# Two transformer layers on one core: another order of the seven products, of the score heads and of TensorE's work in the second attention

## The chip, the cores and the metric

The kernel runs on one core of a Trainium2 chip. The metric is the device time of one execution in microseconds; the time before is the median of three runs. All data are fp32, and every fp32 matmul stands in the trace as two records.

## What is computed

Two pre-norm layers, each an attention and a gated FFN, on x of shape (4, 256, 256): batch B = 4, 256 positions, D = 256. Both attentions have 16 heads of 128.

```python
x = x + L0_attn(layernorm(x))   # sliding window of 128, RMS norm of q and k, RoPE, 8 kv heads
x = x + L0_ffn(layernorm(x))    # silu(x w_gate) * (x w_up), 2 of every 4 units kept, w_down
x = x + L1_attn(layernorm(x))   # causal, no rotation: q, k, v from W_Q, W_K, W_V, out by W_O
x = x + L1_ffn(layernorm(x))    # fwht(silu(x W1) * (x W3)) W2, hidden 1024
```

The change touches the third line and, by a shared generator, the fourth.

## The kernel before

**Steps.** The second attention (`attention1`) works in units of one group of four heads and one batch: unit n = 4g + b, n = 0 to 15. `pipelined` runs three stages over them with lags 0, 1 and 2: in step s it emits `project(s)`, then `score(s - 1)`, then `attend(s - 2)`, so steps run from 0 to 17. After these it calls the functions listed for the step in `behind` (weights of the output projection prepared in steps 1, 5 and 8; FFN work in 0 and from 11 on).

**Project.** Each projection (q and k together as `qk`, and `v`) is a product of 2x2 blocks done with seven block products (Strassen-Winograd) in place of eight. The generator `seven_products` (L643) emits them: product number i adds to one of three PSUM accumulators x, y and z, and after each one an engine reads the accumulator. ScalarE (ACT) copies into the SBUF tiles u0, u1 and u2, or VectorE (DVE) adds a u to the accumulator and writes a block of the result: c11 from z and u0, c12 from y and u2, c22 from x and u1; c21 is ScalarE's copy of x at the end. The accumulators are never cleared between products on the same one, so a product on x must wait until the copy or sum that reads x is through. Below, "x6" is product 6 on accumulator x, and so on. `project1` (L828) runs three such generators in turn, one product of each: qk (four matmuls of 128 columns, L835), v (one of 256, L841) and, for units 4 to 12, `between`: a product of the output projection of the unit four before (`out_by_seven`, matmuls L772, sums L777 on VectorE). These are called the steps with a projection between; steps 0 to 3 and 13 to 15 have none.

**Score and attend.** `score` calls `probabilities` for two pairs of heads. Per head it has two score matmuls (L213 and L214) into a bank, reductions with mask and maximum on VectorE (L216), then by pair the bias nb (L221), four exponentials on ScalarE (L226), the sums' reciprocal rs (L231) and the scaling on GpSimd (POOL, L234). `planes` splits the result into 16-bit planes on POOL (L240) and transposes them by a DMA from SyncE's queue (L249) into plT. `attend` joins the planes into pT (L260: one half on ScalarE, behind c21's copy; the other on VectorE, behind `last_of["sum"]`), multiplies with v (`values`, L268 and L271, into the bank av), and ScalarE copies av into zT (L735). POOL makes sums of zT for the output projection.

**Banks.** The pool `ps1` has four banks in rotation. The four score banks, the two av banks, v's accumulator x and the projection's `po1` share it, so av0 takes a bank that a score had four allocations earlier.

**The second FFN** (`ffn1`) uses `seven_products` too, in eight rounds of half a hidden layer; `gated1` (L906, matmuls L912) puts the down projection's products (`between`) after the fourth and the sixth of the seven products. VectorE makes its weight differences t_gu in steps 14 and on.

**What sets the order.** A scheduler places the instructions of each engine's queue by priorities and its own estimates; source order is its guide and not binding. Each engine then works through its queue in order. In the second attention it had moved part of the scores and av matmuls of steps 1 to 3 and 13 to 15 ahead of products that come earlier in the source: one score head ahead of x4 in steps 1, 3, 13, 14 and 15, and in step 2 three scores ahead of x6 and one ahead of x4, with av matmuls in part before x4 and behind the next step's first product. In steps 4 to 12 TensorE's queue follows the source.

Of the kernel before, what the change touches and what calls it, by code (L numbers as in the profile page):

```python
# [20 lines left out]
F32 = mybir.dt.float32  # L21
# [3 lines left out]
ALU = mybir.AluOpType  # L25
# [3 lines left out]
B, T, D = 4, 256, 256  # L29
# [19 lines left out]
def two_layers(ctx, tc, consts, tables, x, wq, wkv, wo, w_gate, w_up, w_down,  # L49
               w_k, w_q, w_v, w_o, w1, w3, w2, out):  # L50
    nc = tc.nc
# [27 lines left out]
    def page(name):  # L79

        return work.tile([P, 4, T], F32, tag="page", name=name, bufs=8)
# [9 lines left out]
    mask1 = cst[:, C_M1:]  # L91
# [52 lines left out]
    last_of = {}  # L144
# [121 lines left out]
    def values(v0, v1, pT, av):  # L266

        nc.tensor.matmul(  # L268
            av, lhsT=v0, rhs=pT[:, 0:T], start=True, stop=False, skip_group_check=True
        )  # L270
        nc.tensor.matmul(  # L271
            av[:, P:T], lhsT=v1, rhs=pT[:, T : 3 * P], start=False, stop=True,
            skip_group_check=True,
        )
# [21 lines left out]
        xt = xs[b * NT + t]  # L296
        nc.vector.tensor_tensor(xt, po, xt, ALU.add)

    def pipelined(stages, lags, behind, order):


        done, held, depth = {}, {}, max(lags) + 1
        for step in range(B * 4 + depth - 1):
            for k in order:
                n = step - lags[k]
                if 0 <= n < B * 4:
                    held[n] = stages[k](n, held.get(n))
                    if stages[k] is stages[-1]:
                        done[n] = held.pop(n)
            for fn in behind.get(step, ()):  # L310
                fn(done)


    def attention0():
# [328 lines left out]
    def seven_products(product, x, z, y, c11, c12, c21, c22, shape, z_alone=True):  # L643


        u = [late.tile(shape, F32, tag="u", name="u", bufs=4) for _ in range(3)]
        product(y, 5, True)
        nc.scalar.copy(u[1], y)
        yield
        product(x, 1, True)  # L650
        nc.scalar.copy(u[0], x)
        yield
        product(z, 2, z_alone)
        nc.vector.tensor_tensor(c11, z, u[0], ALU.add)
        yield
        product(x, 6, False)
        nc.scalar.copy(u[2], x)
        yield
        product(y, 3, False)
        nc.vector.tensor_tensor(c12, y, u[2], ALU.add)  # L660
        yield
        product(x, 7, False)
        last_of["sum"] = nc.vector.tensor_tensor(c22, x, u[1], ALU.add)
        yield
        product(x, 4, False)
        last_of["copy"] = nc.scalar.copy(c21, x)  # L666
        yield
# [23 lines left out]
    def attention1(finish_ffn0):  # L691
        left = left1

        def project(n, _):
            g, b = divmod(n, 4)
            if b == 1 and 1 <= g < 3:
                load_group1(g + 1)
            held = project1(left[b], gw[g], out_by_seven(n - 4) if 4 <= n < 13 else None)
            if g == 0 and b + 1 < B:
                with tc.issue_after(last_of["sum"].ins):  # L700
                    left[b + 1] = left_of(xn1[b + 1])
            if g == 0 and b + 2 < B:
                xn1[b + 2] = normed(b + 2, by_dma=True)
            return held

        def score(n, held):
            qk, v = held
            ps = [
                probabilities(qk[:, 0], qk[:, 1], (2 * kk, 2 * kk + 1), mask1) for kk in range(2)
            ]  # L710
            return [planes(p, page_of_planes) for p in ps], v

        zTs, kept = {}, {14: (9, 10), 15: (11, 13)}

        def attend(n, held):
            ps, v = held
            for m in kept.get(n, ()):
                out(m, True)(zTs)
            if n in (1, 3, 5, 7):
                zT = late.tile([P, 4, T], F32, tag="zT1", name="zT1", bufs=1)  # L720
            else:
                zT = page("zT1")
            zTs[n] = zT
            for kk in range(2):
                pT = joined(ps[kk], (
                    (
                        (nc.vector.tensor_copy, slice(0, 1), None) if n < 1 else
                        (nc.scalar.copy, slice(0, 1), last_of["copy"])
                    ),
                    (nc.vector.tensor_copy, slice(1, 2), last_of["sum"]),  # L730
                ))
                av = bank([2, T], "av1")
                for j in range(2):
                    values(v[:, 0, 2 * kk + j, :], v[:, 1, 2 * kk + j, :], pT[:, j], av[:, j, :])
                nc.scalar.copy(zT[:, 2 * kk : 2 * kk + 2, :], av)  # L735
            if n < 9:
                z_left[n] = left_of_z(zT, z_sums[:, n % 2])
            return zT

        z_left, w_right = {}, {}  # L740

        def left_of_z(z, s):
            x11, x12, x21, x22 = (
                z[:, 2 * k : 2 * k + 2, t * P : (t + 1) * P] for t in range(2) for k in range(2)
            )
            for i, a, b, op in (
                (0, x21, x22, ALU.add), (1, s[:, 0], x11, ALU.subtract),
                (2, x11, x21, ALU.subtract), (3, x12, s[:, 1], ALU.subtract),
            ):
                nc.gpsimd.tensor_tensor(s[:, i], a, b, op)  # L750
            return x11, x12, s[:, 3], x22, s[:, 0], s[:, 1], s[:, 2]

        def right_of_out(g):
            w, t = gw[g][2], w_sums[:, g % 2]
            w_right[g] = right_of(
                *(w[:, 2 * k : 2 * k + 2, m * P : (m + 1) * P] for k in range(2) for m in range(2)),
                [t[:, i] for i in range(4)],
            )

        def out_by_seven(n):  # L760


            g, b = divmod(n, 4)
            left, right = z_left[n], w_right[g]
            sums = bank([3, P], "po1")
            x, y, z = (sums[:, i, :] for i in range(3))
            for o, i, t, m in (
                (y, 5, 1, 1), (x, 1, 0, 0), (z, 2, 0, 0), (x, 6, 0, 1), (y, 3, 0, 1),
                (x, 7, 1, 1), (x, 4, 1, 0),
            ):  # L770
                for j in range(2):
                    nc.tensor.matmul(  # L772
                        o, lhsT=left[i - 1][:, j, :], rhs=right[i - 1][:, j, :],
                        start=(i == 5 and j == 0), stop=(j == 1), skip_group_check=True,
                    )
                to = xs[b * NT + t][:, m * P : (m + 1) * P]
                nc.vector.tensor_tensor(to, o, to, ALU.add)  # L777
                yield

        def load_ffn1(_):  # L780
            nonlocal w1_sb, w3_sb
            w1_sb = load_ffn(w1, (NC, NF, P), "w1")
            w3_sb = load_ffn(w3, (NC, NF, P), "w3")

        def out(n, kept=False):
            g, b = divmod(n, 4)

            def emit(done):
                if not kept:
                    project_out1(bank([NT, D], "po1"), done[n], gw[g][2], b)  # L790
                else:
                    with tc.issue_after(last_of[1].ins):
                        project_out1(st([P, NT, D], "po1"), done[n], gw[g][2], b)
            return emit

        behind = {step: [lambda _, g=g: right_of_out(g)] for g, step in enumerate((1, 5, 8))}
        behind[0] = [lambda _: finish_ffn0()]
        behind[12] = [load_ffn1]

        def prepare(_):  # L800
            w2h.extend(hadamard(w2_raw))
            w2h[1](_)

        behind.setdefault(11, []).append(prepare)
        for i in range(12):
            behind.setdefault(11 + i // 4, []).append(
                lambda _, i=i: w2h[2][i](last_of["planes"].ins)
            )

        def prepare_ffn1(half):  # L810
            def emit(_):
                with tc.issue_after(last_of["sum"].ins):
                    r_ffn1.append(factors_ffn1(half))
            return emit

        behind.setdefault(14, []).append(prepare_ffn1(0))
        behind.setdefault(15, []).append(out(12))
        behind[16] = behind.get(16, []) + [
            lambda _: xn_f.append(normed(0, by_dma=True)),
            prepare_ffn1(1),  # L820
        ]
        behind[17] = [out(14), out(15)]
        pipelined((project, score, attend), (0, 1, 2), behind, (0, 1, 2))

    def st(shape, name):
        return st_pool.tile(shape, F32, tag="st", name=name)
# [104 lines left out]
    def ffn1():  # L931
# [22 lines left out]
    late = ctx.enter_context(  # L954
        tc.tile_pool(name="late", bufs=2, reuse_waits="tile", side="right")
    )
# [97 lines left out]
```

## Time and profile before

| what | value |
|---|---|
| median of 3 runs (lowest, highest) | 737.86 us (737.40, 738.69) |
| the profiled execution | 738.5 us |
| its span in the trace | 736.7 us |
| first attention and FFN (0 to 352 us): TensorE busy | 345.3 of 352.0 us |
| second attention (352 to 654.6 us): TensorE busy | 300.7 of 302.6 us |
| second FFN (654.6 to 736.7 us): TensorE busy | 79.1 of 82.1 us |
| TensorE clock granted, all three stretches | 1.00 |
| one step with a projection between (431.25 to 449.06) | 17.81 us |

The profile is one execution taken by the hardware profiler. Its page lists the busy time of each engine (PE is the matmuls, PEld the weight loads), the chain of work that ended last, and the costliest groups of instructions. The timeline gives start and length of instructions by engine; a bracket at its end says how long the engine stood idle before and what released it. "L663" is line 663 of the kernel. Ends of matmuls are modelled, so pauses of TensorE are read from start to start.

### The profile page before, as it was taken

The page shows a single profiled execution, that of the slowest core. Times are in us where ns is not written, and L with a number is a line of the kernel's source. Part 1 is how long each engine was busy: PE and PEld are TensorE (multiplying, and loading weights), DVE is VectorE, ACT ScalarE, POOL GpSimd, SP SyncE. Part 2 cuts the span into 40 slices and gives each one's busy share as a digit, 9 for nine tenths or more (in the row PEclk, how much of TensorE's full clock was granted, in tenths as well). Part 3 has the DMA queues.
Part 4 walks back from the last instruction along what each step waited for, and adds up shares of the span by engine and source line. Part 5 has one row for each costly group of instructions (what it writes and reads, how often), then busy time and mean ns, then how long its engine had stood idle before and what let it go on. Part 6 is the DMA issues. An engine that isn't in the chain of part 4 may idle for free.

```text
span 736.7 us, 11967 instructions
## 1 busy us (share of the span) xinstructions
PE 725.1 (98%) x4020; PEld 597.1 (81%) x4020; DVE 485.5 (66%) x1459; ACT 407.6 (55%) x983; POOL 369.8 (50%) x525
## 2 busy tenths in 40 slices
PE   9999999999999999999999999999999999999998
PEld 5556576666666778888998999999998999899997
DVE  6999877888887537987855755575453566464443
ACT  2487887667768952222265555555555666434332
POOL 1588878897799631011127544464446665520000
PEclk9999999999999999999999999999999999999999
DMA  8732344425445545001114433442233522401100
GB/s 323 298 65 51 58 92 82 92 52 93 89 79 98 84 105 182 16 14 24 58 21 82 120 58 44 86 116 44 44 73 44 158 44 44 88 13 23 23 14 30
DMA packets 138350, 57.54 MB, mean 78 GB/s; under 512 B 131504, under 2 KB 133680, under 8 KB 137520
## 3 DMA queue, kind: packets, MB, share of 16 engines
q1 hardware_dynamic: 138288, 56.77, 33.7%
q8 instruction: 32, 0.52, 0.3%
q14 instruction: 30, 0.25, 0.1%
HBM read 22.94 MB, written 1.05 MB: 33 GB/s over the span
## 4 chain that ended last, share of the span: by engine, by line
PE 70%; POOL 9%; DVE 8%; issue 7%; ACT 3%; DMA 2%; SPq 0%; POOLq 0%; DVEq 0%; ACTq 0%
PE pj L446 10%; PE po_f L595 8%; PE pgu L550 8%; PE po L292 7%; PE qk_x L835 4%; PE sc L214 4%; PE gu_x L912 4%; PE av L394 3%; POOL p L234 3%; POOL pl L240 3%; PE po L772 3%; PE qk_y L835 2%; PE sc L213 2%; PE v_x L841 2%; PE gu_y L912 2%
## 5 line engine op out<-in xcount | busy, mean ns | idle before, releaser
L234 POOL TENSOR_SCALAR p<-p,rs 128x128 f32<-128x128 f32 (+1 forms) x256 | 115.9, 470 | 129.2 <-DVE rs L231 124.0
L240 POOL TENSOR_SCALAR pl<-p 128x1536 uint16<-128x1536 uint16 x64 | 94.2, 1472 | 4.5 <-POOL p L234 0.5
L260 ACT COPY pT<-plT 128x1536 uint16<-128x1536 uint16 (+1 forms) x60 | 86.4, 1495 | 12.3 <-DMA plT<-pl 12.3
L216 DVE CUSTOM_DVE_ANT_0 p<-sc,cst 128x128 f32<-128x128 f32 (+1 forms) x256 | 78.9, 352 | 9.4 <-PE sc L214 7.3
L226 ACT ACTIVATE p<-p,nb,r 128x128 f32<-128x128 f32 (+1 forms) x128 | 68.3, 535 | 20.1 <-DVE nb L223 20.1
L226 ACT ACTIVATE p<-p,nb 128x128 f32<-128x128 f32 (+1 forms) x128 | 56.4, 441 | 11.9 <-DVE nb L221 11.9
L446 PE MATMUL pj<-wq,xnT 128*128 128x512 f32 x128 | 61.2, 597 | 1.1 <-DVE qT L508 1.1
L446 PE MATMUL pj<-wkv,xnT 128*128 128x512 f32 x128 | 60.1, 592 | 0.0
L292 PE MATMUL po<-wo,zT 128*128 128x256 f32 x256 | 57.9, 379 | 0.0
L456 ACT ACTIVATE sq<-pj 128x512 f32<-128x512 f32 (+1 forms) x64 | 30.9, 489 | 42.6 <-DVE qc L451 42.2
L292 PEld LDWEIGHTS po<-wo,zT 128*128 128x128 f32 x256 | 48.3, 190 | 7.0 <-ACT kT L519 0.6
L156 POOL TENSOR_SCALAR ve<-mv 128x2 f32<-128x2 f32 (+1 forms) x17 | 4.4, 258 | 95.5 <-DVE mv L152 95.0
L446 PEld LDWEIGHTS pj<-wkv,xnT 128*128 128x128 f32 x128 | 24.3, 190 | 30.2 <-issue 28.5
L666 ACT COPY qk<-qk_x 128x512 f32<-128x512 f32 x16 | 9.4, 586 | 64.7 <-PE qk_x L835 61.1
L451 DVE TENSOR_TENSOR qs<-pj,sin_s 128x512 f32<-128x512 f32 (+1 forms) x64 | 35.3, 552 | 13.5 <-PE pj L446 12.9
L446 PEld LDWEIGHTS pj<-wq,xnT 128*128 128x128 f32 x128 | 23.7, 191 | 24.3 <-issue 20.1
L777 DVE TENSOR_TENSOR x<-po,x 128x128 f32<-128x128 f32 x63 | 18.0, 286 | 35.8 <-PE po L772 35.8
L268 PE MATMUL av<-pT,v 128*128 128x256 f32 x128 | 38.6, 383 | 1.8 <-DVE nb L221 1.1
L240 POOL TENSOR_SCALAR qpl<-qc 128x1024 uint16<-128x1024 uint16 x20 | 28.8, 1450 | 19.1 <-PE av L398 8.3
L214 PE MATMUL sc<-kT,qT 128*128 128x256 f32 x128 | 38.3, 381 | 0.0
L214 PE MATMUL sc<-qk 128*128 128x256 f32 x128 | 38.2, 380 | 0.0
L489 POOL TENSOR_TENSOR r<-ve,mhalf 128x12 f32<-128x12 f32 x16 | 36.6, 2288 | 0.8
(165 smaller groups left out, 1858.0 us busy)
## 6 DMA issues: line engine op xcount, KB each, us to landing
w<-in_w_dram SPq DMA_DIRECT2D x3, 1024.0 KB, 4.7
wq<-in_wq_dram SPq DMA_DIRECT2D x4, 512.0 KB, 7.6
wkv<-in_wkv_dram SPq DMA_DIRECT2D x4, 512.0 KB, 8.2
wo<-in_wo_dram SPq DMA_DIRECT2D x4, 512.0 KB, 10.2
w_qk<-in_w_q_dram SPq DMA_DIRECT2D x4, 512.0 KB, 4.2
w_qk<-in_w_k_dram SPq DMA_DIRECT2D x4, 512.0 KB, 6.0
w_v<-in_w_v_dram SPq DMA_DIRECT2D x4, 512.0 KB, 7.1
w_o<-in_w_o_dram SPq DMA_DIRECT2D x4, 512.0 KB, 5.6
```

Of the source, the lines that this page charges most:

```text
L214: nc.tensor.matmul(sc[:, P : 3 * P], lhsT=q[:, P:T], rhs=k, start=True, stop=True)
L216: last_of["mx"] = nc.vector.tensor_tensor_reduce(out=p[:, j, cols], in0=sc[:, cols], in1=mask[:, cols], scale=1.0, scalar=-3.0e38, op0=ALU ...
L226: last_of["exp"] = nc.scalar.activation(p[:, j, cols], p[:, j, cols], AF.Exp, bias=nb[:, j, i : i + 1], scale=SCALE1 if rq is None else rq ...
L234: nc.gpsimd.tensor_scalar(p[:, j, cols], p[:, j, cols], rs[:, j, i : i + 1], 1.0, ALU.mult, ALU.mult)
L240: last_of["planes"] = nc.gpsimd.tensor_scalar(o, i, 1.0, 1.0, ALU.mult, ALU.mult)
L260: copy(words.rearrange("p (n w) -> p w n", w=2), halves[:, :, js].rearrange("p w j n -> p w (j n)"),)
L292: nc.tensor.matmul(po, lhsT=zTs[hd // 4][:, hd % 4, t * P : (t + 1) * P], rhs=w[:, hd, :], start=(hd == 0), stop=(hd == n - 1),)
L446: last_of[0] = nc.tensor.matmul(pj, lhsT=xnT[:, c, t * P : (t + 1) * P], rhs=w[:, g, c, :], start=(c == 0), stop=(c == NC - 1),)
L550: nc.tensor.matmul(o[:, j, :], lhsT=w[:, c, f0 + j, :], rhs=xnT[:, c, :], start=(c == 0), stop=(c == NC - 1),)
L595: nc.tensor.matmul(pos[b][t], lhsT=hs[n][:, j, t * P : (t + 1) * P], rhs=w[:, 4 * gc + j, :], start=(gc == 0 and j == 0), stop=(gc == 1 an ...
L835: last_of[1] = nc.tensor.matmul(o[:, j, :], lhsT=wqk[i - 1][:, j // 2, j % 2, :], rhs=x[i - 1], start=(first and j == 0), stop=True, skip_ ...
L912: nc.tensor.matmul(o[:, j, :], lhsT=r[j // 2][i - 1][:, j % 2, :], rhs=x[i - 1], start=(first and j == 0), stop=True, skip_group_check=True,)
```

## The change

1. `seven_products`: the order of products goes from 5, 1, 2, 6, 3, 7, 4 (accumulators y x z x y x x) to 1, 5, 6, 3, 7, 2, 4 (x y x y x z x). c11's sum, and with it `last_of["sum"]`, comes sixth. The u tiles of qk and v get tags of their own, three tiles each, in place of one tag with four. `out_by_seven` goes to the same order.
2. `score` takes the head pairs (1, 3) and (0, 2) in place of (0, 1) and (2, 3); `attend` indexes v by the new heads and copies av into every second head of zT.
3. `pipelined` gets `in_order`; the second attention gives (1, 18), which holds TensorE to source order (`tc.manual_schedule`) in steps 1 to 17. The other engines stay with the scheduler.

The queues of the changed kernel, as built: nothing moves on any engine in the first attention and FFN, and SyncE's queue is the same throughout. On TensorE each of steps 1 to 17 is seven products, four scores, four av, in this order. ScalarE and VectorE have their copies and sums in the new order; where the scheduler of before set the reductions of a score between two pT copies (as at 587.50), both pT copies now come first, and in step 16 the reductions come ahead of the pT copies. POOL moves two small norm operations near the end.

```diff
@@ -296,19 +296,26 @@
         xt = xs[b * NT + t]
         nc.vector.tensor_tensor(xt, po, xt, ALU.add)
 
-    def pipelined(stages, lags, behind, order):
+    def pipelined(stages, lags, behind, order, in_order=(0, 0)):
 
 
         done, held, depth = {}, {}, max(lags) + 1
-        for step in range(B * 4 + depth - 1):
-            for k in order:
-                n = step - lags[k]
-                if 0 <= n < B * 4:
-                    held[n] = stages[k](n, held.get(n))
-                    if stages[k] is stages[-1]:
-                        done[n] = held.pop(n)
-            for fn in behind.get(step, ()):
-                fn(done)
+        def steps(numbers):
+            for step in numbers:
+                for k in order:
+                    n = step - lags[k]
+                    if 0 <= n < B * 4:
+                        held[n] = stages[k](n, held.get(n))
+                        if stages[k] is stages[-1]:
+                            done[n] = held.pop(n)
+                for fn in behind.get(step, ()):
+                    fn(done)
+
+        first, last = in_order
+        steps(range(first))
+        with tc.manual_schedule(engines={mybir.EngineType.PE}):
+            steps(range(first, last))
+        steps(range(last, B * 4 + depth - 1))
 
 
     def attention0():
@@ -643,15 +650,13 @@
     def seven_products(product, x, z, y, c11, c12, c21, c22, shape, z_alone=True):
 
 
-        u = [late.tile(shape, F32, tag="u", name="u", bufs=4) for _ in range(3)]
-        product(y, 5, True)
-        nc.scalar.copy(u[1], y)
-        yield
+        tag = "u" if len(shape) == 3 else "uv"
+        u = [late.tile(shape, F32, tag=tag, name="u", bufs=3) for _ in range(3)]
         product(x, 1, True)
         nc.scalar.copy(u[0], x)
         yield
-        product(z, 2, z_alone)
-        nc.vector.tensor_tensor(c11, z, u[0], ALU.add)
+        product(y, 5, True)
+        nc.scalar.copy(u[1], y)
         yield
         product(x, 6, False)
         nc.scalar.copy(u[2], x)
@@ -660,7 +665,10 @@
         nc.vector.tensor_tensor(c12, y, u[2], ALU.add)
         yield
         product(x, 7, False)
-        last_of["sum"] = nc.vector.tensor_tensor(c22, x, u[1], ALU.add)
+        nc.vector.tensor_tensor(c22, x, u[1], ALU.add)
+        yield
+        product(z, 2, z_alone)
+        last_of["sum"] = nc.vector.tensor_tensor(c11, z, u[0], ALU.add)
         yield
         product(x, 4, False)
         last_of["copy"] = nc.scalar.copy(c21, x)
@@ -706,7 +714,7 @@
         def score(n, held):
             qk, v = held
             ps = [
-                probabilities(qk[:, 0], qk[:, 1], (2 * kk, 2 * kk + 1), mask1) for kk in range(2)
+                probabilities(qk[:, 0], qk[:, 1], heads, mask1) for heads in ((1, 3), (0, 2))
             ]
             return [planes(p, page_of_planes) for p in ps], v
 
@@ -731,8 +739,9 @@
                 ))
                 av = bank([2, T], "av1")
                 for j in range(2):
-                    values(v[:, 0, 2 * kk + j, :], v[:, 1, 2 * kk + j, :], pT[:, j], av[:, j, :])
-                nc.scalar.copy(zT[:, 2 * kk : 2 * kk + 2, :], av)
+                    hd = 2 * j + 1 - kk
+                    values(v[:, 0, hd, :], v[:, 1, hd, :], pT[:, j], av[:, j, :])
+                nc.scalar.copy(zT.rearrange("p (j m) t -> p m j t", m=2)[:, 1 - kk], av)
             if n < 9:
                 z_left[n] = left_of_z(zT, z_sums[:, n % 2])
             return zT
@@ -765,13 +774,13 @@
             sums = bank([3, P], "po1")
             x, y, z = (sums[:, i, :] for i in range(3))
             for o, i, t, m in (
-                (y, 5, 1, 1), (x, 1, 0, 0), (z, 2, 0, 0), (x, 6, 0, 1), (y, 3, 0, 1),
-                (x, 7, 1, 1), (x, 4, 1, 0),
+                (x, 1, 0, 0), (y, 5, 1, 1), (x, 6, 0, 1), (y, 3, 0, 1), (x, 7, 1, 1),
+                (z, 2, 0, 0), (x, 4, 1, 0),
             ):
                 for j in range(2):
                     nc.tensor.matmul(
                         o, lhsT=left[i - 1][:, j, :], rhs=right[i - 1][:, j, :],
-                        start=(i == 5 and j == 0), stop=(j == 1), skip_group_check=True,
+                        start=(i == 1 and j == 0), stop=(j == 1), skip_group_check=True,
                     )
                 to = xs[b * NT + t][:, m * P : (m + 1) * P]
                 nc.vector.tensor_tensor(to, o, to, ALU.add)
@@ -820,7 +829,7 @@
             prepare_ffn1(1),
         ]
         behind[17] = [out(14), out(15)]
-        pipelined((project, score, attend), (0, 1, 2), behind, (0, 1, 2))
+        pipelined((project, score, attend), (0, 1, 2), behind, (0, 1, 2), (1, B * 4 + 2))
 
     def st(shape, name):
         return st_pool.tile(shape, F32, tag="st", name=name)
```

## The prediction

> **What bounds the kernel now.** I read the page first, then the waits of TensorE, the chain of waits around a middle step, and the timeline at the places where TensorE waits. Sections 1 and 4 of the page:
>
> ```profile
> PE 725.1 (98%) x4020; PEld 597.1 (81%) x4020; DVE 485.5 (66%) x1459; ACT 407.6 (55%) x983; POOL 369.8 (50%) x525
> PE 70%; POOL 9%; DVE 8%; issue 7%; ACT 3%; DMA 2%; SPq 0%; POOLq 0%; DVEq 0%; ACTq 0%
> ```
>
> TensorE is busy for 98% of the span. The change adds and removes no TensorE work, so it can only win back pauses between matmuls. I measured these in the trace: start of one matmul record to start of the next, less the 112, 218 or 431 ns that records of 128, 256 or 512 columns take when nothing holds them. Lost that way: 9.5 us before 352 us (untouched), 3.1 us in the second attention (352 to 654), 0.4 us in the second FFN. So at most about 3.5 us, 0.5%, can be gained; more can be lost. A measurement of this kernel can tell about 0.2%, 1.5 us.
>
> The steady pause. First the chain of waits in step 4 (start, length):
>
> ```profile
> 440.11 0.89 PE qk_x L835 x8
> ...
> 441.88 1.06 PE qk_x L835 x8
> ```
>
> and the timeline beside it:
>
> ```profile
> 441.04 0.69 DVE L663 TENSOR_TENSOR qk<-qk_x,u 128x512 f32<-128x512 f32 x1 [0.48 <-PE qk_x L835]
> ...
> 441.78 0.74 PEld L835 LDWEIGHTS qk_x<-xnT,t_qk 128*128 128x128 f32 x6
> 441.78 0.82 PE L835 MATMUL qk_x<-xnT,t_qk 128*128 128x128 f32 x5
> ```
>
> In the chain the first row is x7, the second x4, which adds onto the same accumulator. x4 waits until VectorE's c22 sum (L663) has read it: 441.04 + 0.69 = 441.73. Its weight load begins only then, at 441.78, with the matmul. So x4 holds 1.06 us where x7 holds 0.89.
>
> The start of the second attention (timeline, steps 2 and 3):
>
> ```profile
> 381.52 1.28 ACT L226 ACT_TABLE_LOAD   x1
> ...
> 382.81 0.40 ACT L226 ACTIVATE p<-p,nb 128x128 f32<-128x128 f32 x1
> ...
> 385.49 1.05 PE L835 MATMUL qk_z<-xnT,w_qk 128*128 128x128 f32 x8
> ...
> 386.33 0.56 ACT L648 COPY u<-qk_y 128x512 f32<-128x512 f32 x1
> ...
> 386.38 0.39 PE L213 MATMUL sc<-qk 128*128 128x128 f32 x2
> ...
> 397.07 0.70 PE L268 MATMUL av<-pT,v 128*128 128x256 f32 x2 [1.07 <-DVE nb L221]
> ```
>
> The eight exponentials of step 1's scores, held by the table load, stand ahead of step 2's first u copy. In before the scheduler sets scores (386.38) where TensorE would have waited. The one large pause comes later, at 397.07.
>
> The tail (timeline, step 16):
>
> ```profile
> 629.48 0.60 DVE L260 COPY pT<-plT 128x768 uint16<-128x768 uint16 x1 [3.02 <-DMA plT<-pl]
> 629.97 0.28 DVE L216 CUSTOM_DVE_ANT_0 p<-sc,cst 128x128 f32<-128x128 f32 x1
> ...
> 635.22 1.03 ACT L260 COPY pT<-plT 128x768 uint16<-128x768 uint16 x1
> ...
> 636.30 0.70 PE L268 MATMUL av<-pT,v 128*128 128x256 f32 x2 [0.45 <-ACT pT L260]
> ```
>
> VectorE stands 3.02 us before a pT copy whose transpose has not landed; the last scores' reductions wait behind it, the exponentials after them, and ACT's pT copy behind those. TensorE pauses 0.6 us at 636.30 and 0.3 us at 646.25.
>
> **The change part by part.** The profiled run took 738.5 us, 1.8 of them outside its span of 736.7, and 0.64 more than the median of 737.86. I sum against 738.5 and take off 0.64.
>
> *New product order, steps 4 to 12.* z2 now lies between x7 and x4. In these steps a product with its share of the output projection takes 0.89 + 0.43 + 0.44 = 1.77 us, and c22's two sums end 0.7 to 1.0 us after x7, so x4 waits no more. The other reuses (x6 after x1's copy, y3 after y5's, x7 after x6's) are also one product apart: 1.77 us against a copy of 0.56 to 0.59. Each of the nine steps wins 0.17: -1.53. The bounds are 0 and -1.6. The u tiles (two tags of three for one of four) and the later release of w21 cost nothing: a u is read two or three products after it is written, and the next group's weights land steps ahead; without that cover a step would wait about one copy, 0.6.
>
> A rule to weigh: the Trainium skill, page "TensorE: Matmul & The Clock Gate", opening table, says that the queue pulls weight loads ahead of matmuls in flight. Then the load should have been hidden during x4's wait, each step would lose only the 0.07 until 441.78, and the gain would be nearer 0.6 than 1.5. The row above shows otherwise, and I go by the row.
>
> *Start, steps 1 to 3.* TensorE is now held to source order, so step 2's x6 comes third, at 382.84 + 2 x 1.33 = 385.49, with no scores before it. It needs the copy of x1's sum, which stands behind the eight exponentials: start 386.33 at the latest, 0.3 sooner if the table load moves up with x4, plus 0.56. So x6 waits 1.2 to 1.5. Then VectorE's queue has the pT copy of attend(0), whose transpose lands at 391.87, ahead of c22, and x4 waits 0 to 0.9. At the end of step 2 the second pT pair (landing 395.01) is ahead of the reductions of scores(1), and the first av waits 0 to 0.9. I take 1.3 + 0.8 + 0.5 = 2.6 for these; the 1.3 at 397.07 (1.23, and 0.10 after it) goes. Net +1.3, bounds 0 and +2.0.
>
> *Step 8.* VectorE builds four t_v and w_sums for the next group ahead of four output sums L777. Before lost 0.27 and 0.10 there. The new list puts two more such operations ahead: +0.2, bounds 0 and +0.4.
>
> *Steps 13 to 15 (no output projection between products).* VectorE's list now runs c11's two sums (1.1 us from the end of z2), two pT copies (0.6 each alone, 1.47 and 1.13 at 586.14 and 588.05, beside POOL), in steps 14 and 15 two t_gu (about 0.4 each), and then the reductions of the first scores (0.7), whose bank av0 takes. av0 is due 1.33 + 2.6 = 3.93 us after z2. The list ends 3.0 to 5.3 us after it. Before, one score stood ahead of x4 and its reduction got in early; the loss there was 0.37. I take +0.4, nearer the short copies, which are the usual ones; bounds -0.3 and +1.7.
>
> *Tail, steps 16 and 17.* With TensorE in source order the lists of VectorE put the reductions of scores(15) ahead of the pT copy that waited 3.02 us. The exponentials come about 3 us earlier and ACT's pT copy with them; most of 0.7 + 0.4 goes: -0.8, bounds 0 and -1.1.
>
> *Scores with heads 1 and 3 first; the strided zT copy.* In steady state the scores read the step before's qk, long complete, so no wait ends sooner. The zT copy keeps its 512 elements (0.52 us) in pieces of 256 and hides under the next products: 0; bounds +/-0.1.
>
> *Second FFN.* It uses the same generator. x7 and x4 part (-0.2 to -0.3 in the first two halves), but x6 and y3 wait for copies of 0.58 us with nothing between products (46 ns each at x6 now): +0.1, bounds -0.2 and +0.4. POOL's moved ve and rstd operations (0.19 each) have nobody waiting.
>
> Sum: -1.53 + 1.3 + 0.2 + 0.4 - 0.8 + 0.1 = -0.3. 738.5 - 0.3 - 0.64 = 737.5 (rounded from 737.56).
>
> **The rivals.** *Gain (0.33).* The start costs nothing net: its new pauses only take the place of the 1.3 at 397.07, since the transposes land when they did, and the tail gives its 0.8. Then -1.5 + 0 + 0.1 + 0.2 - 0.8 + 0 = -2.0, or 735.9; with the full tail and nothing in steps 8 to 15, -2.7: 735.2. For it: the landings (391.87, 395.01) do not depend on TensorE's order, so an early pause shortens a later one. Against: the exponentials at 382.81 are as fixed.
>
> *Slower (0.28).* TensorE in order has nothing to put before a late ACT or VectorE. The mechanism is one: reductions behind pT copies make the exponentials late, and these hold av0 and the next step's u0. Its place is steps 3, 13, 14 and 15, which have no projection between products. Its price is 0.6 (the pause at 636.30, the nearest row of a late copy) to 1.2 (397.07) each, 2.4 to 4.8 in place of my 0.4. It decides once the pT copies take over 1.1 us each. With 2.4 to 3.2 the sum is +1.7 to +2.5: 739.6 to 740.4.
>
> *The change doesn't do what it says (0.03 of the next figure).* The scheduler may already give nearly this order, or x4 may wait as before for something else on VectorE, so that the -1.53 does not come; with the rest at zero the time stays at 737.9.
>
> **How the numbers follow.** The forecast, a sum near zero, has 0.39, the last rival in it; its own range is 736.4 to 739.3. Gain has 0.33, slower 0.28. The range for 8 in 10 reaches into both: 735.3 to 740.0. Faster by over 0.2% (under 736.4): the gain case, 0.33, and 0.02 of the forecast's edge, 0.35. Slower (over 739.3): 0.28 and 0.02, 0.30. The same: 0.35.
>
> **What would show it.** Right: in steps 4 to 12 x4 holds 0.89 in the chain, and a step takes 17.64 in place of 17.81 us; a pause of 1.2 to 1.5 us before x6 in step 2, with ACT's exponentials as its cause; 397.07's counterpart under 0.9; no 3 us stand of VectorE before the tail's pT copy. Wrong: x6 unheld in step 2 (then the gain case), or av waits over 0.6 in each of steps 13 to 15 (then the slower one). A clock below 1.00 after the start's pauses would void the sum.

## The result, and the profile after

The changed kernel takes 740.74 us (740.41 to 741.22, 6 runs) beside 737.83 for the kernel before: ratio 1.0038, 95% interval 1.0025 to 1.0051. It is slower by 2.9 us, and 740.74 lies above the range of the prediction. The profiled execution took 740.41 us with a span of 738.5.

On the page TensorE is as busy as before, so again the pauses have to be looked at one by one:

```profile
PE 724.2 (98%) x4020; PEld 596.0 (81%) x4020; DVE 484.1 (66%) x1459; ACT 407.2 (55%) x983; POOL 375.0 (51%) x525
```

The waits of TensorE (us in total, times, longest) have four rows that before did not have:

```profile
PE po L781 <- POOL p L234: 1.9, 2, 1.0
PE av L268 <- DVE mx L216: 1.8, 2, 1.5
...
PE qk_x L844 <- ACT u L656: 1.3, 1, 1.3
...
PE qk_x L844 <- DVE qk L668: 0.6, 1, 0.6
```

The last two are the start (x6 and x4 of step 2), which was forecast. The first two were not, or not in their size.

The steady pause is gone. In the chain of waits in step 5 (431.67 to 449.31), x4 holds what x7 holds, and z2 (qk_z) lies between; the step takes 17.64 us, as forecast. (The prediction's rows at 440.11 and 441.88 are of step 5 too, though it calls it step 4.)

```profile
438.76 0.89 PE qk_x L844 x8
...
440.53 0.89 PE qk_z L844 x8
...
442.30 0.89 PE qk_x L844 x8
```

Steps 4 and 8, the first row of the waits. Timeline of step 4 (VectorE, then TensorE):

```profile
412.10 0.69 DVE L647 TENSOR_TENSOR t_qk<-w_qk 128x512 f32<-128x512 f32 x1 [1.03 <-DMA w_qk<-in_w_k_dram]
...
416.47 0.28 DVE L786 TENSOR_TENSOR x<-po,x 128x128 f32<-128x128 f32 x1
...
416.89 0.68 PE L781 MATMUL po<-w_sums,z_sums 128*128 128x128 f32 x4 [0.93 <-POOL p L234]
```

The table of waits names POOL, but the projection's second product starts 0.14 us after VectorE's sum L786 of the first has ended (416.75), and so do the other pauses of this kind, in step 8. That sum stands behind eight weight differences for the next group, and the first of these waited 1.03 us for a weight load, w_k. The loads of w_q and w_k were issued 6.7 and 5.8 us before the step's start (412.70); in the kernel before, 8.1 and 7.7. SyncE's queue in step 3 shows what stands ahead of them:

```profile
401.31 4.61 SPq L249 DMA_TRANSPOSE plT<-pl  x2
405.98 0.85 SPq L685 DMA_DIRECT2D w_qk<-in_w_q_dram  x1
406.88 0.44 SPq L686 DMA_DIRECT2D w_qk<-in_w_k_dram  x1
```

Both transposes are issued by 405.92, and z2, the last product that reads the old w_qk, ran until 405.86 (404.81 and 1.05): the load follows both within 0.12 us. Its own issue takes 0.85 us here, 0.33 in the kernel before. In step 8 the first sum held TensorE for 0.29 us and the second, behind two slow t_v, for 1.24:

```profile
487.53 2.10 DVE L647 TENSOR_TENSOR t_v<-w_v 128x256 f32<-128x256 f32 x2
...
490.33 0.28 DVE L786 TENSOR_TENSOR x<-po,x 128x128 f32<-128x128 f32 x1
...
490.76 0.68 PE L781 MATMUL po<-w_sums,z_sums 128*128 128x128 f32 x4 [1.00 <-POOL p L234]
```

Steps 13 to 15, the second row. Timeline of step 14 (POOL, VectorE, TensorE):

```profile
599.37 5.49 POOL L893 TENSOR_TENSOR w_b<-w 128x512 f32<-128x512 f32 x4
...
602.23 2.91 DVE L647 TENSOR_TENSOR t_gu<-w 128x256 f32<-128x256 f32 x2
605.06 0.58 DVE L260 COPY pT<-plT 128x768 uint16<-128x768 uint16 x1
605.54 0.27 DVE L216 CUSTOM_DVE_ANT_0 p<-sc,cst 128x128 f32<-128x128 f32 x1
...
606.31 0.67 PE L268 MATMUL av<-pT,v 128*128 128x256 f32 x2 [1.49 <-DVE mx L216]
```

POOL runs the four Hadamard additions of this step (L893) until 604.86. Beside them two t_gu take 2.91 us; alone a t_gu takes 0.42 (607.83 in the same trace). The first score reduction starts only at 605.54, 3.5 us after its score's first matmul at 602.04, and av0, which takes that score's bank, waits. In step 13 the two pT copies took 3.05 us beside such additions (586.36). In step 15 POOL ran none and the copies took 0.6 each; there the first copy waited for its transpose until 618.45.

The start and the tail went as forecast:

```profile
385.34 1.16 PE L844 MATMUL qk_x<-xs,t_qk 128*128 128x128 f32 x8 [1.28 <-ACT u L656]
...
391.52 1.16 PE L844 MATMUL qk_x<-xnT,t_qk 128*128 128x128 f32 x8 [0.61 <-DVE qk L668]
...
635.88 1.04 ACT L260 COPY pT<-plT 128x768 uint16<-128x768 uint16 x1
...
637.11 0.59 PE L268 MATMUL av<-pT,v 128*128 128x256 f32 x2
```

x6 of step 2 waits for ScalarE's u copy behind the eight exponentials. In the tail the pT copy of ScalarE now ends before av0 begins, not between the two av.

### The profile page after: what moved, and what is told of

The parts are those of the page before. It is cut to its first block, busy times and chain, and to the rows that moved or that the text cites. A ratio compares the mean times of both kernels' runs of the same rounds, so it can differ in the third digit from the quotient of the medians.

```text
span 738.5 us, 11898 instructions
## 1 busy us (share of the span) xinstructions
PE 724.2 (98%) x4020; PEld 596.0 (81%) x4020; DVE 484.1 (66%) x1459; ACT 407.2 (55%) x983; POOL 375.0 (51%) x525
## 3 DMA queue, kind: packets, MB, share of 16 engines
HBM read 22.94 MB, written 1.05 MB: 32 GB/s over the span
## 5 line engine op out<-in xcount | busy, mean ns | idle before, releaser
L234 POOL TENSOR_SCALAR p<-p,rs 128x128 f32<-128x128 f32 (+1 forms) x256 | 115.9, 472 | 129.1 <-DVE rs L231 129.1
L240 POOL TENSOR_SCALAR pl<-p 128x1536 uint16<-128x1536 uint16 x64 | 96.7, 1511 | 4.1
L786 DVE TENSOR_TENSOR x<-po,x 128x128 f32<-128x128 f32 x63 | 18.0, 286 | 35.5 <-PE po L781 35.5
L240 POOL TENSOR_SCALAR qpl<-qc 128x1024 uint16<-128x1024 uint16 x20 | 29.2, 1474 | 18.0 <-PE av L405 8.2
```

What stands on the lines that cost most here:

```text
L234: nc.gpsimd.tensor_scalar(p[:, j, cols], p[:, j, cols], rs[:, j, i : i + 1], 1.0, ALU.mult, ALU.mult)
L240: last_of["planes"] = nc.gpsimd.tensor_scalar(o, i, 1.0, 1.0, ALU.mult, ALU.mult)
```

## The experiments

Each was compared with the kernel before on the same chip. Its median there was 737.81 us beside the first four kernels, 738.65 beside the next four and 738.75 to 738.79 beside the last ones, so the numbers to compare are the differences. The changed kernel's is +2.91.

**One part at a time.** The first three kernels are the kernel before with one part of the diff each: the product order, the last line's `in_order`, the head pairs.

> The kernel before with the first part of the change alone (order of the seven products in both generators, u tags); TensorE's order is left to the scheduler. Theory Q (what was lost is lost in VectorE's queue, and the new product order alone brings most of it): in this build the scheduler leaves source order only in step 2, so step 2 has no 1.4 us pause before x6, x4's 0.17 is gone in steps 4 to 12 (-1.5), the pauses before the output projection's matmuls in steps 4 and 8 are there (over 2 us together, +2.2) and so are those before the first av in steps 13 to 15 (about 2.5 together, +2.2): 739.5 to 740.7 us. Rival S (source order on TensorE is what costs): the order alone gives the steady gain, 736.0 to 737.0.

Measured: 739.23, +1.42 (ratio 1.0022, 1.0012 to 1.0032). The time is a little under theory Q's 739.5, and the pauses are where it put them: 2.45 us in steps 4 and 8 (0.22 in step 4, 2.23 in step 8), 2.54 in steps 13 to 15, 0.42 at the start. Rival S falls: the product order alone makes the kernel slower. Of step 4's 1.16 us in the changed kernel, though, it brings only a small part.

> The kernel before with the third part alone (TensorE in source order in steps 1 to 17, old product order and heads). Theory Q: the pause before x6 in step 2 and those before av in steps 13 to 15 are there, since no score head stands ahead of x4 any more; the steps 4 and 8 lose no more than before (under 0.5 together), x4 keeps its 0.17, the tail wins 0.8: 739.3 to 740.8. Rival S: all of the change's loss and not its gain, 741 or more. Rival O (the product order is the whole loss): 737.5 to 738.2.

Measured: 743.17, +5.36 (1.0074, 1.0062 to 1.0087), more than theory Q allowed. It lies in rival S's range, but not for S's reason: steps 4 and 8 lost 0.92 together, not the changed kernel's 2.69. Rival O falls. The miss is the old order without the scheduler's help: where no projection lies between products, x4 directly behind x7 loses 0.61, not 0.17, in each of steps 1, 3, 13, 14 and 15, and 1.43 in step 2. The score head that the scheduler of before had put between x7 and x4 was hiding that. The first av of step 14 lost 1.65 here too. The tail's pauses are 0.34, as in the changed kernel.

> The kernel before with the second part alone (heads 1 and 3 first, zT written in pieces of 256). Theory Q: nothing waits for it, 737.3 to 738.3. Rival H (the strided zT copies or the heads hold something): 738.5 or more.

Measured: 738.23, +0.42 (1.0006, 0.9997 to 1.0015): no difference that can be told.

**Steps 4 and 8.** The diff of the first run, shortened (its comments name the steps in whose source the calls stand):

```diff
-        gw[g] = (right_of(qk ...), right_of(v ...), o)
+        if g < 2: gw[g] = (qk_right(), v_right(), o); return
+        with tc.issue_after(last_of["mx"].ins):      # step 5 or 9
+            first = qk_right()
+        def rest():                                  # called in step 6 or 10
+            with tc.issue_after(last_of["mx"].ins):
+                gw[g] = (first, v_right(), o)
```

> The changed kernel, but VectorE makes the weight differences of groups 2 and 3 later: t_qk behind the score reductions of steps 5 and 9, t_v behind those of steps 6 and 10, in place of the start of steps 4 and 8. Theory Q: the output sums L786 no longer stand behind operations that wait for a weight load, so the pauses in steps 4 and 8 (1.16 and 1.24 + 0.29) vanish and nothing else moves: 2.2 to 2.7 us less than the changed kernel, 738.0 to 738.6. Rival P (POOL holds the output projection, as the table of waits names it): no change, 740.7.

Measured: 738.24, +0.43 (1.0008, 0.9999 to 1.0017): 2.5 us less than the changed kernel, and no pause over 0.06 us is left between 393 and 556 us. As built, t_qk runs one step earlier than the expectation says, behind the reductions of steps 4 and 8 (from 428.88 in step 4, which begins at 413.01), and t_v behind those of steps 5 and 9. VectorE in step 4 (timeline) now waits for TensorE, not TensorE for it:

```profile
414.18 0.18 DVE L231 RECIPROCAL rs<-sm 128x4 f32<-128x4 f32 x1 [1.58 <-ACT p L226]
414.98 0.29 DVE L799 TENSOR_TENSOR x<-po,x 128x128 f32<-128x128 f32 x1 [0.62 <-PE po L794]
```

POOL's work was not touched, so the name in the table of waits was wrong, and rival P falls.

> The changed kernel, with z2 back in third place in steps 3 and 7 alone, the last steps of groups 0 and 1, so that the raw weights w21 are read out as early as before. Theory L (the pauses in steps 4 and 8 come from the next weights, whose load starts later because z2 reads w21 sixth): the loads of w_q and w_k start about 1.3 us earlier in step 3 and 1.8 in step 7, VectorE waits for neither, the pauses of steps 4 and 8 (1.16 and 1.24 + 0.29) fall to under 0.8 together, while x4 of steps 3 and 7 loses 0.6 and 0.17 again: 739.2 to 740.0 us where the changed kernel has 740.7. Rival V (VectorE's list alone, the t operations standing ahead of L786 whenever the weights land): loads earlier, but over 1.5 us of pauses stay and the time is 740.7 or more.

Measured: 741.38, +2.63 (1.0033, 1.0020 to 1.0045), 0.3 less than the changed kernel; 0.7 to 1.5 was expected. The load of w_q was issued 7.4 us ahead of step 4 (6.7 in the changed kernel) and 10.4 ahead of step 8 (7.7). The pauses fell from 1.16 to 0.53 in step 4 and from 1.52 to none in step 8, so in step 8 how late the weights come does set them. But VectorE still waited for w_k, 0.40 in step 4 and 1.45 at the end of step 7, there with a t_qk now ahead of the score reductions, and the first av of step 7 lost 0.79. The wait moved in the queue; it did not go. In step 3 SyncE's queue gave little: its two transposes were through only at 407.36 and the first load went at 407.41, 7.8 us after the step's start as in the changed kernel. It gained on step 4 only because x4's wait of 0.61 made step 3 longer, so this run does not single out z2 as the cause in step 4.

**The start.** The diff is `(1, B * 4 + 2)` to `(4, B * 4 + 2)`.

> The changed kernel with TensorE's source order from step 4 on only; in steps 1 to 3 the scheduler chooses, and in this build it puts three scores of step 2 ahead of x6 and one ahead of x4. Theory Q: the two pauses of step 2 (1.54 and 0.87) shrink to under 0.5 together, the pauses of steps 4, 8 and 13 to 15 stay: 738.2 to 739.2 us. Rival (the start only shifts: what is not lost there is lost at the next fixed landing): within 0.5 of the changed kernel, 740.3 or more.

Measured: 739.19, +0.54 (1.0006, 0.9997 to 1.0015), 2.4 less than the changed kernel. The start's pauses fell from 2.42 to 0.43, and those of step 4 from 1.16 to 0.24: VectorE began the weight differences 1.5 us ahead of the step (0.6 in the changed kernel) and waited for no load. Here SyncE's transposes of step 3 were issued by 403.25, 2.1 us ahead of w_q's load, and w_k's load left 6.4 us before the step (5.8 in the changed kernel). So step 4's pause takes both parts of the change: the product order alone gives 0.22, source order alone 0.44, the two together 1.16. Step 8 gave some back: 1.97 in place of 1.52.

**Steps 13 to 15.** The diffs are `11 + i // 4` to `11 + max(0, i - 2) // 2` in the list of POOL's additions, and `last_of["sum"]` to `last_of["mx"]` in `prepare_ffn1`.

> The changed kernel, with POOL's twelve Hadamard additions handed out 4, 2, 2, 2, 2 over five steps in place of 4, 4, 4 over three. Theory Q: VectorE's pT copies and t_gu in steps 13 to 15 take 1.5 us each only beside these additions and 0.6 and 0.4 without; with two a step they end before the pT copies, these take about 0.6 again, and the pauses before the first av (0.55, 1.72, 0.26) fall to under 0.6 together: 738.6 to 739.4 us. Rival T (the two t_gu ahead of the reductions and the queue's order are enough): the pause of step 14 stays over 1 us, 740 or more.

Measured: 739.75, +1.10 (1.0014, 1.0005 to 1.0023), 1.8 less than the changed kernel. VectorE's list is the same, its times in step 14 are not:

```profile
602.46 0.59 DVE L260 COPY pT<-plT 128x768 uint16<-128x768 uint16 x1
602.94 0.74 DVE L647 TENSOR_TENSOR t_gu<-w 128x256 f32<-128x256 f32 x2
603.61 0.59 DVE L260 COPY pT<-plT 128x768 uint16<-128x768 uint16 x1
```

Two t_gu take 0.74 where they took 2.91, and 0.07 us is left of the 2.53 lost in these steps. This is shown: in steps 13 and 14 POOL's additions beside VectorE were the cause, and the queue's order alone was not.

> The changed kernel, with the weight differences t_gu of the second FFN put behind the last score reduction of the step in place of behind c11's sum. Theory Q: only step 14 gains, its pause falls from 1.72 to about that of step 13 (0.5), since the pT copies beside POOL still take 1.5 each: 739.3 to 739.9 us. Rival T: all three pauses go, 738.2 to 738.7.

Measured: 740.50, +1.85 (1.0025, 1.0016 to 1.0034), 1.1 less than the changed kernel. Without the two t_gu between them the pT copies of step 14 took 0.88 and 0.81 and its pause went altogether, a little more than expected; those of steps 13 and 15 stayed (0.52 and 0.65). In step 14 either repair was enough.

**All repairs.**

> The changed kernel with the four repairs at once: later weight differences of groups 2 and 3, source order from step 4 on only, POOL's additions spread, t_gu behind the reductions. If the losses add up as theory Q has them, the second attention loses under 1 us in all, and the time is that of the run with the later weight differences (738.2) less 2.0 for the start and 2.5 for steps 13 to 15: 733.4 to 735.0 us, faster than both kernels. If removed pauses come back elsewhere: 736 or more.

Measured: 735.08, -3.57 (0.9951, 0.9938 to 0.9963): faster than both kernels.

> The changed kernel with all four repairs, but heads 0 and 1 first and zT written in one piece as before. Theory Q: the heads' order and the pieces of zT count for nothing: within 0.5 us of the repaired kernel (735.1 beside a before of 738.65, ratio 0.9951). Rival H: the time differs by over 1 us, either way.

Measured: 735.36, -3.39 (0.9952, 0.9938 to 0.9966): the heads count for nothing here either.

> The kernel before, with three of the four repairs (later weight differences of groups 2 and 3, POOL's additions spread, t_gu behind the reductions) and nothing of the change. It shows what of the repaired kernel's gain is the change's own. Theory Q: the repairs take away only what before loses in the same places, 0.44 in steps 4 and 8 and 0.37 in step 14: 0.3 to 1.0 us less than before, so that over 2 us of the repaired kernel's gain need the change. Rival: the repairs are worth over 2 us by themselves.

Measured: 741.90, +3.15 (1.0039, 1.0027 to 1.0052): neither. The pauses of steps 4, 8 and 14 went, but in the tail both of ScalarE's pT copies of unit 14 now stood ahead of the exponentials of unit 15. The whole chain behind them (scaling, planes, transpose, copy) came late, and the last av waited 3.1 us. Windows of the trace (width, then busy us of PE, PEld, DVE, ACT and POOL with counts, the granted clock, the share and rate of DMA) show what followed:

```profile
646.00:647.00 1.00, 0.00 (x0) 0.00 (x0) 0.08 (x1) 0.10 (x1) 0.00 (x0) 1.00 1.11 214
647.00:648.00 1.00, 0.00 (x0) 0.00 (x0) 1.00 (x3) 0.97 (x2) 0.00 (x0) 0.55 0.46 86
...
649.00:653.00 4.00, 4.00 (x13) 3.34 (x12) 2.58 (x11) 1.31 (x3) 0.90 (x2) 0.50 0.00 0
...
654.00:655.00 1.00, 1.00 (x6) 0.87 (x6) 0.00 (x0) 0.00 (x0) 0.00 (x0) 1.00 0.00 0
```

The clock fell to half before the pause ended, at 647.1, and stayed there until 653.9, for 6.8 us; the matmuls in it lost 2.8 us more. The profiled run was the slowest of the five (740.22 to 743.16). The execution of 740.22 kept a mean granted clock of 1.000, so the fall of the clock does not come every time; without it this kernel is still slower than before's 738.75, by the pause as it seems, but no trace of that execution is kept.

> The kernel before with the same three repairs and TensorE's source order in steps 16 and 17 alone; old product order, old heads, the scheduler's order in steps 1 to 15. In the run without that order both pT copies of unit 14 stood ahead of the last exponentials on ScalarE, the last av waited 3.1 us, and the granted clock fell to 0.50 behind it. Theory Q: the tail now goes as in the repaired changed kernel (no pause over 0.5, clock 1.00), and with the repairs' 0.8 and the tail's 0.8 the time is 1.2 to 2.2 us under before; the change's own product order is then worth the remaining 1.5 to 2.3 of the repaired kernel's 3.6. Rival: the early reductions do not come of TensorE's order, the long pause stays, and the time is over before's.

Measured: 737.09, -1.70 (0.9979, 0.9970 to 0.9988). Clock 1.00, no long pause in the tail. So of the repaired kernel's 3.6 us some 1.7 come from the three repairs and the order of the tail, and some 1.9 from the rest: product order, heads and source order in steps 4 to 15. By place the rest is 1.53 at x4 and 0.89 at the start, less 0.37 in the tail and 0.2 in the second FFN. The run with the product order alone has both gains (0 at x4, 0.42 at the start), so they are put down to that order.

**The sums.** Pauses of the second attention by place, in us, from the starts of the matmul records as in the prediction (only those over 0.06), and what their total says beside the measured difference:

| kernel | start, 1-3 | x4, 4-12 | steps 4, 8 | 13-15 | tail | total less before's | measured |
|---|---|---|---|---|---|---|---|
| before | 1.34 | 1.53 | 0.44 | 0.37 | 1.14 | | |
| changed | 2.42 | 0 | 2.69 | 2.53 | 0.34 | +3.2 | +2.9 |
| product order alone | 0.42 | 0 | 2.45 | 2.54 | 0.97 | +1.6 | +1.4 |
| source order alone | 3.59 | 1.53 | 0.92 | 3.48 | 0.34 | +5.3 | +5.4 |
| later weight differences | 2.41 | 0 | 0 | 2.66 | 0.34 | +0.6 | +0.4 |
| free start | 0.43 | 0 | 2.20 | 2.45 | 0.34 | +0.6 | +0.5 |
| POOL spread | 2.41 | 0 | 2.76 | 0.07 | 0.34 | +0.8 | +1.1 |
| t_gu later | 2.40 | 0 | 2.57 | 1.17 | 0.43 | +1.8 | +1.9 |
| all repairs | 0.45 | 0 | 0 | 0.07 | 0.71 | -3.6 | -3.6 |
| before, repaired, tail in order | 1.34 | 1.53 | 0 | 0 | 0.34 | -1.6 | -1.7 |

(The total of source order alone holds 0.27 more before the first av of step 7.) The totals agree with the measured differences within 0.3 us, so the places add up. Each repair takes its own pause and hardly gives it back, but for the free start, which also took most of step 4's and added 0.45 in step 8.

## Why the prediction was wrong, point by point

The forecast sum was -0.3; the trace has +3.2 in the second attention and +0.2 in the second FFN. The sign of no term was wrong. Steps 4 and 8 together came out 2.0 us over their term of +0.2, steps 13 to 15 1.8 over theirs of +0.4; both are losses behind operations in VectorE's queue that ended late.

*x4 in steps 4 to 12:* -1.53 forecast, -1.53 measured. Going by the row, and not by the rule on weight loads, was right: a waiting x4 lost its 0.10 for the load after the wait again wherever the old order ran (0.51 + 0.10 in the source-order run).

*Start:* +1.3 forecast, +1.08 measured (1.54 before x6, 0.87 before x4, no pause before av).

*Step 4:* the step that failed is "the later release of w21 cost nothing ... the next group's weights land steps ahead". They do not: VectorE makes their differences at the end of step 3 as soon as the load allows, and in the changed kernel it could start only 0.6 us before step 4, with the output sums behind it. The later release is only part of the reason. Alone it costs 0.15 us here (0.22 against 0.07 before); the rest came with source order in steps 1 to 3, after which SyncE's transposes stood directly ahead of the load. The prediction had no term for that. How much of the pause is z2's and how much the transposes' stays open, since in the changed kernel the two end within 0.1 us. I had named the price of lost cover as one copy, 0.6; it was 1.09 more than before in step 4. I had seen the queue of step 8 and not that step 4 has the same one.

*Step 8:* +0.2 forecast, bounds 0 and +0.4; measured +1.15 (0.37 before, 1.52 after). Here the later release of w21 is the cause: the product order alone has the pause (2.23), source order alone hardly (0.48), and z2 in third place takes it away (0.79 came back before an av of step 7). In addition two t_v took 2.10 us at 487.53, with POOL's scaling and planes (L234, L240) beside them; what these cost was not tested by itself.

*Steps 13 to 15:* +0.4 forecast, bounds -0.3 and +1.7; measured +2.16. The queue was read rightly (pT, t_gu, pT, then reductions, av0 waiting for the bank), and I had the rows of 1.47 and 1.13 us for a pT copy beside POOL. I then took the short copies, "the usual ones", for steps in which POOL runs its additions at just that time, and t_gu at 0.4 each where it took 1.46. The bound was too low by the prediction's own list: with its late end of 5.3 us against av0's 3.93, steps 14 and 15 would lose 1.4 each and step 13 some 0.5, about +2.9 over before, not +1.7. The slower rival named this queue and place, and its 739.6 to 740.4 is close to the 740.74, but partly by luck: its deciding point (copies over 1.1 us each) was met in step 13 alone, in step 14 the two t_gu took the time, step 3 lost nothing, av0 waited for the score reductions and not for the exponentials that it names, and it had nothing of steps 4 and 8. It had a chance of 0.28, and the range was cut at 740.0 through the middle of it.

*Tail:* -0.8 forecast, -0.80 measured. *Heads and zT:* 0 forecast, +0.4 with an interval that holds 0. *Second FFN:* +0.1 forecast, +0.2 measured (of POOL's two norm operations only ve takes the 0.19 that the prediction gives for both; rstd takes 0.70).

The Trainium skill has a line that bears on the term of steps 13 to 15, though without a price: page "GPSIMD Engine Reference", section Specifications, says that GpSimd's SBUF interfaces are shared with VectorE, with contention for VectorE's instructions in a two-port mode or with two SBUF inputs. The runs agree with such a contention beside POOL's additions: pT copies 0.6 to 1.5 us, t_gu (two SBUF inputs) 0.37 to 1.46, while a score reduction, which reads PSUM and one SBUF input, kept 0.27 and 0.42 beside the same additions (587.50 and 587.70 in the trace of before). No run shows in which mode a pT copy runs.

## What to carry to other kernels

When a change shifts an engine's queue by a microsecond, look at what now runs beside it on the engine that slows it (here GpSimd beside VectorE), and price each operation by the row with that neighbour, not by the usual one. A buffer that is read some products later can delay the load behind it, and the price is paid by whatever stands behind the first user of that load in its queue. Taking a scheduler's freedom away also takes away the fillers that it had put into waits: before doing so, list what each out-of-order instruction was hiding.

## What the runs showed of the hardware that was not expected

A pause of TensorE of 3.1 us was enough to halve the granted clock, from 647.1 to 653.9 us: it fell 2.0 us after the last matmul before the pause (645.08). The Trainium skill, page "TensorE: Matmul & The Clock Gate", Part 1, gives one idle window of about 3.4 us for this; the run's pause was a little under that. It did so in the profiled execution; the five means run from 0.995 to 1.000. At the end of the kernel, where TensorE has no more work, the clock records of the traces fall 2.0 to 5.1 us after the last matmul, so a pause of 3.1 us may or may not meet the fall. The pauses of up to 1.7 us in the other runs left the mean at 0.997 to 1.000.

The releaser in a table of waits was wrong by an engine: it named POOL's p where VectorE's sum held the matmul. The distance of 0.14 us from the end of L786 to the start, in each of the pauses, was the better witness.

Between profiles the untouched first half loses 7.9 to 9.8 us in pauses, so that single spans differ by nearly 2 us; pauses by place repeat far better (x6 of step 2: 1.44 to 1.45 in five runs), and only they made so small a change readable.
